# A chunked delta-rule block: chunks of 64 tokens with two sequences in one tile, instead of chunks of 128 tokens

## The chip, the cores and the metric

The kernel runs on one core of a Trainium2 chip. A core has five engines with a queue each: TensorE (PE in the profile; its weight loads are PEld), VectorE (DVE), ScalarE (ACT), GpSimd (POOL) and SyncE (SP), which issues the DMAs here. The metric is the device time of one launch in microseconds, the median of the runs; less is better. All data is float32.

## The reference, cut to what matters

The input x has 8 sequences of 1024 tokens with 128 features. The block is a layernorm, a gated delta-rule attention with 16 heads (keys of 64, values of 128), a layernorm and a residual, and then a small feed-forward part with a token shift. The attention is a recurrence over the tokens, one state S of 64 x 128 per sequence and head:

```python
q = causal_conv_silu(x @ Wq.T, conv_q)      # 4 taps, then l2_norm; k likewise
v = causal_conv_silu(x @ Wv.T, conv_v)
alpha = exp(-exp(A_log) * softplus(x @ Wa.T + dt_bias)); beta = 2 * sigmoid(x @ Wb.T)
def step(S, q_t, k_t, v_t, a_t, b_t):
    kS = einsum('bhd,bhdv->bhv', k_t, S)
    S = a_t * (S - b_t * einsum('bhd,bhv->bhdv', k_t, kS)) + einsum('bhd,bhv->bhdv', k_t, v_t)
    return S, einsum('bhdv,bhd->bhv', S, q_t)
o = rms_norm(o) @ Wo.T
x = x + layernorm(o); x = x + layernorm(ffn(layernorm(x)))
```

## The kernel before, in words

The recurrence is done in chunks of 128 tokens. Inside a chunk the effect of the tokens on each other is a triangular matrix of 128 x 128 per head, whose inverse (`tt`) is formed; between chunks only S is carried. A *unit* is one sequence, half of its tokens (four chunks, 512 tokens) and a group of four heads; there are 8 x 2 x 4 = 64 units, and a tile is one chunk of a unit (256 tiles).

The work is written as generators, one for each stage, that yield before each small part:

- `begins` loads x, normalises and transposes it (`xnT`), and computes the decays (`eg`, `ed`, `ee`, `al`); `keys` and `values` compute seven projections of 512 tokens a unit and convolve them (`conv`: ScalarE copies the product to `pb` and scales it into `acc`, GpSimd keeps the three edge tokens, VectorE adds three taps); `directs` computes the fourth value head by four shifted products that accumulate.
- `lengths` computes norms; `products` loads the decay rows broadcast over the partitions (`at`, `egb`), makes the decay matrix by a scan on VectorE, multiplies keys by keys and queries, and forms `mt` and `at`; `decays` scales the queries on GpSimd.
- `gathers`, `blocks`, `scatters` and `levels` invert the triangular matrix: 16 x 16 blocks on GpSimd (by way of DMAs through DRAM), then on TensorE from 16 to 32, from 32 to 64, and from 64 to 128 (three bursts over `tn`, `mt`, `x64`, `tt`).
- `prepares` transposes the keys, scales them into `kc` and `kd`, and forms `pT` from `kc` and `tt`. `steps` runs the recurrence: `tt` by values into PSUM, plus `pT` by S; ScalarE copies that to `w`; `kd` by `w` updates S on VectorE; queries by S plus `at` by `w` is the output. `norms` copies and scales the output; `projects` multiplies by Wo and ends with the feed-forward part (`ending`).

`Flow.run` (line 177) orders the parts at build time: among the parts whose inputs and buffers are there it takes the one that could start soonest by a small cost table (`Engine.cost`, line 245), and breaks ties by a position that each stage is given (the list at the end: stage, parts per unit, offset). The engines then run the emitted order, each its own queue in sequence; a wait at the head of a queue holds all behind it. All emitted instructions have line 234 in the profile, so groups are told apart by tile names. PSUM is two tiles of two banks (`pair`) and four of one (`bank`); a request for a bank may be given half of a pair, which then is not free for anything else.

Of the kernel before, what the change touches and what calls it, by code (L numbers as in the profile page):

```python
# [19 lines left out]
NP = G // 2  # L20
CU = 4
TU = CU * P
NB = CU * G
NVT = 1
NPAIR = 2
# [9 lines left out]
class Flow:  # L35
# [16 lines left out]
    def __init__(self, nc):  # L52
        self.now = dict(PE=0.0, DVE=0.0, ACT=0.0, POOL=0.0, SP=0.0)
        self.free, self.wrote, self.read = {}, {}, {}
        self.kinds, self.work = {}, [0.0, 0.0]
        self.of = {}
        self.speed, self.window, self.used = 1.0, self.WINDOW, [0.0, 0.0]
        self.pe, self.ve = Engine(self, "PE", nc.tensor), Engine(self, "DVE", nc.vector)
        self.ac, self.po = Engine(self, "ACT", nc.scalar), Engine(self, "POOL", nc.gpsimd)
        self.sp = Engine(self, "SP", nc.sync)  # L60

    @staticmethod
    def region(ap):
# [3 lines left out]
        if ap.space == PSUM:  # L67
            return ap.tensor.name, (0, P, ((0, 1),))
        pitch, parts = ap.ap[0][0], ap.ap[0][1]
        starts, n = [ap.offset % pitch if pitch else ap.offset], 1  # L70
        for s, k in sorted(([s, k] for s, k in list(ap.ap)[1:] if s and k > 1), key=lambda x: x[0]):
            if s <= n or len(starts) * k > 32:
                n = s * (k - 1) + n
            else:
                starts = [x + s * i for i in range(k) for x in starts]
        p0 = ap.start_partition()
# [69 lines left out]
    def give(self, kind, tile_):  # L146
        if tile_.space == PSUM:
            kind, tile_ = self.of.pop(tile_.tensor.name, (kind, tile_))
# [5 lines left out]
    def open(self, kind):  # L154

        have = [(kind, t) for t in self.free.get(kind, ())]
        if kind == "bank" and not have:
            have = [("pair", t) for t in self.free.get("pair", ())]
        return have

    def take(self, kind):
        have = sorted(self.open(kind), key=lambda x: self.ends(x[1]))
        of, t = have[0]
        self.free[of] = [x for x in self.free[of] if x.tensor.name != t.tensor.name]
        if t.space == PSUM:
            self.of[t.tensor.name] = of, t
            if of != kind:
                t = t[:, 0:512]
        return t

    def when_free(self, kind, n, eng):
        have = self.open(kind)
        if len(have) < n:
            return None
        return sorted(self.ends(t, eng) for _, t in have)[n - 1]

    def run(self, streams):
# [6 lines left out]
        while waiting:  # L184
            could = []
            for k, (s, (eng, reads, takes, when, spare)) in enumerate(waiting):
                if when is not None and not when():
                    continue
                if spare > len(self.free["bank"]) + len(self.free["pair"]):
# [34 lines left out]
class Engine:  # L224


    def __init__(self, flow, name, eng):
        self.flow, self.name, self.eng = flow, name, eng
# [16 lines left out]
    def cost(self, op, outs, ins, args, kw):  # L245
# [7 lines left out]
        if self.name == "PE":  # L253
# [8 lines left out]
            if k <= 64 and m <= 64:  # L262
                return 0.105, (0.64, 0.04)
# [34 lines left out]
def kernel(  # L298
# [36 lines left out]
    NC = T // P  # L335
    NH = NC // CU

# [6 lines left out]
    psums = []  # L344
    for kind, n, width in (("pair", NPAIR, 1024), ("bank", 8 - 2 * NPAIR, 512)):
        for i in range(n):
            psums.append(ps.tile([P, width], F32, tag=f"{kind}{i}", name=f"{kind}{i}"))
            give(kind, psums[-1])
# [5 lines left out]
    ident = const.tile([P, G, P], F32, tag="ident", name="ident")  # L354
    for i in range(G):
        make_identity(nc, ident[:, i, :])
    ident1 = ident[:, 0, :]
# [5 lines left out]
    )  # L363
    below = const.tile([P, P], F32, tag="below", name="below")
# [5 lines left out]
    ones = const.tile([P, DK], F32, tag="ones", name="ones")  # L370
    nc.gpsimd.memset(ones, 1.0)
    one = ones[:, 0:1]
# [50 lines left out]
    stock("tn", 1, [P, NB, 2 * BL])  # L423
# [8 lines left out]
    Ss = [mem.tile([P, NP, DV], F32, tag=f"S{g}", name=f"S{g}") for g in range(NG)]  # L432
    edge = mem.tile([P, NT - NG * NVT, KW - 1], F32, tag="edge", name="edge")
    x2T = mem.tile([P, 1 + TU], F32, tag="x2T", name="x2T")

    stock("xnT", 2, [P, KW - 1 + T])
    stock("xs", 1, [P, CU, D])
    for kind, n in (("z", 1), ("e", 1), ("la", 1), ("al", 1), ("nbeta", 2), ("eg", 2), ("ed", 2)):
        stock(kind, n, [P, NC, H])
    stock("ee", 2, [P, NC, H // 2])  # L440
    stock("rows", 1, [NC * H, 2, P])
    stock_dram("rowd", 2, [2, NC * H, P])
# [11 lines left out]
    stock("mt", 2, [P, NB, P])  # L454
# [4 lines left out]
    stock("pb", 2, [P, KW - 1 + TU])  # L459
    stock("vT", 1, [P, TU])  # L460
    stock("at", 9, [P, G, P])
    stock("egb", 2, [P, NP, P])
    stock("kd", 2, [P, G, DK])
    stock("kc", 2, [P, G, DK])
    stock("pT", 3, [P, NP, P])
    stock("xc", 1, [P, NB, BL])
    stock("x64", 1, [P, 2 * G, 2 * BL])
# [15 lines left out]
    def weights():  # L483
# [20 lines left out]
        yield part("SP", mt=2)  # L504
        first, second_ = take("mt"), take("mt")
# [20 lines left out]
        give("mt", first)  # L526
# [50 lines left out]
        give("mt", second_)  # L577

    units = [(b, hf, g) for b in range(B) for hf in range(NH) for g in range(NG)]
# [22 lines left out]

    def begins():
        for b in range(B):
            yield part("SP", xnT=1, rowd=1,
                       when=lambda: prog["keys"] >= (b - 1) * NH * NG + 3 or b == 0)
            xnT, rowd = take("xnT"), take("rowd")
            po.memset(xnT[:, : KW - 1], 0.0)
            for c0 in range(0, NC, CU):
# [3 lines left out]
                sy.dma_start(  # L613
                    xs, x[b, c0 * P : (c0 + n) * P].rearrange("(c p) d -> p c d", p=P)
                )
# [13 lines left out]
                ac.copy(xnT[:, KW - 1 + c0 * P : KW - 1 + (c0 + n) * P], pt[:, : n * P])  # L629
                give("bank", pt)  # L630
                give("xs", xs)

# [3 lines left out]
            for c in range(NC):  # L636
                o = KW - 1 + c * P
                pe.matmul(ab[:, c], xnT[:, o : o + P], wabT, start=True, stop=True)
# [7 lines left out]
            ac.activation(nbeta, ab[:, :, 1, :], AF.Tanh, scale=0.5)  # L646
# [18 lines left out]
            for par in range(2):  # L665
                pe.matmul(
                    pg[par * DK : (par + 1) * DK, 2 * n : 2 * n + n // 2].rearrange("p (c r) -> p c r", c=NC),
                    ones, byp[:, :, :, par], start=True, stop=True,
                )
            yield part("ACT", pg)  # L670
            ac.activation(eg.rearrange("p c h -> p (c h)"), pg[:, 0:n], AF.Exp)
            ac.activation(ed.rearrange("p c h -> p (c h)"), pg[:, n : 2 * n], AF.Exp)
            ac.activation(ee.rearrange("p c r -> p (c r)"), pg[:, 2 * n : 2 * n + n // 2], AF.Exp)
            ac.activation(al, la, AF.Exp)
# [3 lines left out]
            po.memset(al[0:1], 0.0)  # L678
            pr = take("bank")
            yield part("PE", al)  # L680
            for i, t in enumerate((al, eg)):
                pe.transpose(
                    pr[:n, i * P : (i + 1) * P], t.rearrange("p c h -> p (c h)"), ident1
                )
# [3 lines left out]
            sy.dma_start(rowd.rearrange("k n t -> n k t"), rows)  # L688
# [3 lines left out]
            gs[b] = dict(xnT=xnT, nbeta=nbeta, eg=eg, ed=ed, ee=ee, rowd=rowd)  # L692

    def heads_of(u, t):

        b, hf, g = u
        return t[:, hf * CU : (hf + 1) * CU, g * G : (g + 1) * G]


    def conv(n, u, done, m=None):  # L700
# [3 lines left out]
        yield part("PE", bank=1, spare=2, when=lambda: len(done) < 2 and m in loaded)  # L704
        pp = take("bank")
        xT = gs[b]["xnT"][:, KW - 1 + hf * TU : KW - 1 + (hf + 1) * TU]
        pe.matmul(pp, wT[:, m, :], xT, start=True, stop=True)
        yield part("ACT", pp, acc=1, pb=1)
        acc, pb = take("acc"), take("pb")
        ac.copy(pb[:, KW - 1 :], pp)  # L710
        ac.activation(acc, pp, AF.Copy, scale=taps[:, n, KW - 1 : KW])
        give("bank", pp)

        yield part("POOL", *([pb] if hf < NH - 1 else []))
        if hf:
            po.tensor_copy(pb[:, : KW - 1], edge[:, m, :])
        else:
            po.memset(pb[:, : KW - 1], 0.0)
        if hf < NH - 1:
            po.tensor_copy(edge[:, m, :], pb[:, TU:])  # L720
        for j in range(KW - 1):
            yield part("DVE", acc, pb)
            ve.scalar_tensor_tensor(
                acc, pb[:, j : j + TU], taps[:, n, j : j + 1], acc, ALU.mult, ALU.add
# [15 lines left out]
    def lengths():  # L740
        for n, u in enumerate(units):
# [6 lines left out]
            for pr in range(NP):  # L748
                for i in range(2):
# [3 lines left out]
                    ac.activation(qk[:, pr, i], acc, AF.Silu)  # L753
# [50 lines left out]
    def rows():  # L804
        for n, u in enumerate(units):
# [9 lines left out]
            for h in range(G - NVT):  # L815
# [3 lines left out]
                ac.activation(vT, acc, AF.Silu)  # L819
# [16 lines left out]
    def directs():  # L836
        for n, u in enumerate(units):
            b, hf, g = u
            a = st[n]
            for c in range(CU if NVT else 0):  # L840
                t0 = hf * TU + c * P
# [3 lines left out]
                for j in range(KW):  # L845
                    pe.matmul(
                        pv[:, : NVT * DV], xnT[:, t0 + j : t0 + j + P],
                        wv[:, g, j].rearrange("p h v -> p (h v)"), start=j == 0, stop=j == KW - 1,
                    )
# [13 lines left out]
    def decays():  # L863
        for _ in range(len(units) * CU):
# [5 lines left out]
            st[n]["decayed"] = st[n].get("decayed", 0) + 1  # L870
# [5 lines left out]
    def products():  # L876
        def fetch(n, c):
            b, hf, g = units[n]
            yield part("SP", at=1, egb=1, when=lambda: b in gs)
            n0 = (hf * CU + c) * H + g * G  # L880
            at, egb, rowd = take("at"), take("egb"), gs[b]["rowd"]
            sy.dma_start(
                at.rearrange("p h t -> p (h t)"),
                rowd.rearrange("k n t -> k (n t)")[0:1, n0 * P : (n0 + G) * P]
                .broadcast_to([P, G * P]),
            )
            for par in range(2):
                src = rowd[1:2, n0 + par : n0 + G : 2, :]
                sy.dma_start(egb[par * DK : (par + 1) * DK], src.broadcast_to([DK, NP, P]))
# [3 lines left out]
        for n, u in enumerate(units):  # L893
            a = st[n]
            for c in range(CU):
                if ahead is None:
# [4 lines left out]
                atf = at.rearrange("p h t -> p (h t)")  # L901
                ve.tensor_tensor_scan(
                    atf, atf, ident.rearrange("p h t -> p (h t)"), 0.0, ALU.mult, ALU.add
                )
                ahead = None
                k = n * CU + c + 1
# [3 lines left out]
                yield part("PE", pair=1, spare=2, when=lambda: prog["keys"] > n, **takes)  # L910
# [3 lines left out]
                tok = slice(c * P, (c + 1) * P)  # L914
                mt = a["mt"][:, c * G : (c + 1) * G]
# [510 lines left out]
```

## Time and profile before

| | |
|---|---|
| median of 3 runs | 3778.35 us (3777.87 to 3783.65) |
| profiled execution, span | 3779.1 us |
| TensorE busy | 3435.4 us (91%), mean granted clock 0.949 |
| VectorE busy | 2688.5 us (71%) |
| GpSimd busy | 2404.3 us (64%) |
| ScalarE busy | 2311.7 us (61%) |
| DMA | 186.28 MB, mean 49 GB/s |

The page has no other time for the profiled execution than its span. Busy time is the union of an engine's instructions; it says how full an engine is, not that it waits for nothing. "out<-in" names the tile written and those read; for TensorE the numbers before the shape are the rows and columns of the array that the instruction uses (64*128: half of the rows). The mean of one instruction includes its way through the array, so it overlaps with its neighbours; busy time over count, or the step between starts, is what it takes.

### The profile page before, as it was taken

Reading aid. Unit: us, or ns where it says so; the run is one execution under the profiler, and the core shown is the slowest. Engines: PE = TensorE matmul, PEld = TensorE weight load, DVE = VectorE, ACT = ScalarE, POOL = GpSimd, SP = SyncE. Lnnn points to the kernel's source line nnn. Section 1 sums busy time; section 2 is a strip of 40 time slices with the busy share of each in tenths; the row PEclk is TensorE's granted clock in tenths of the full one; section 3 lists DMA queues with packets and bytes.
Section 4 is the critical chain, followed back from the end, with each engine's and each line's share of the span. In section 5 each row is a group of like instructions: output and inputs, shape, how many; then the busy total and the mean of one; then the engine's idle time right before and its main releaser. Section 6 shows DMA issues by size and latency. Waiting matters only on the chain.

```text
span 3779.1 us, 126912 instructions
## 1 busy us (share of the span) xinstructions
PE 3435.4 (91%) x52848; PEld 2646.7 (70%) x52848; DVE 2688.5 (71%) x5021; ACT 2311.7 (61%) x5779; POOL 2404.3 (64%) x4369
## 2 busy tenths in 40 slices
PE   6899998999999999998998989999998989989996
PEld 3677776777777776776766767767776767667775
DVE  5776767677777777866777677777767777777752
ACT  4566656666657666666656656566565666566652
POOL 4666667567666666666566566666666656576662
PEclk8899999999999999999999999999999989999997
DMA  3221222222222222221222222222222222222210
GB/s 80 56 53 39 54 45 49 54 45 55 49 55 46 57 50 43 56 53 40 54 44 53 52 42 53 47 54 51 51 45 55 49 41 60 44 48 53 49 39 11
DMA packets 713151, 186.28 MB, mean 49 GB/s; under 512 B 573152, under 2 KB 679040, under 8 KB 712576
## 3 DMA queue, kind: packets, MB, share of 16 engines
q1 hardware_dynamic: 712576, 178.17, 22.9%
q8 instruction: 415, 6.80, 0.8%
q14 instruction: 160, 1.31, 0.1%
HBM read 138.18 MB, written 23.07 MB: 43 GB/s over the span
## 4 chain that ended last, share of the span: by engine, by line
PE 63%; DVE 10%; POOL 7%; ACT 7%; SPq 6%; issue 5%; DMA 3%; POOLq 0%; DVEq 0%; ACTq 0%
PE bank L234 38%; PE pair L234 25%; SPq L234 6%; DVE acc L234 5%; POOL nb L234 3%; POOL tmp L234 2%; DMA nb<-md 2%; ACT acc L234 1%; DVE x L234 1%; ACT tt L234 1%; DVE at L234 1%; ACT L234 1%; ACT pb L234 1%; POOL vr L234 1%; ACT junk L234 1%
## 5 line engine op out<-in xcount | busy, mean ns | idle before, releaser
L234 DVE SCALAR_TENSOR_TENSOR acc<-pb,taps,acc 128x512 f32<-128x512 f32 x1344 | 1076.1, 806 | 158.2 <-POOL pb L234 64.9
L234 POOL TENSOR_TENSOR vr<-vr,r 128x128 f32<-128x128 f32 (+1 forms) x448 | 353.9, 791 | 252.5 <-ACT vr L234 247.0
L234 PE MATMUL bank<-xnT,wT 128*128 128x512 f32 x892 | 492.4, 641 | 14.8 <-ACT tt L234 8.7
L234 POOL TENSOR_TENSOR nb<-nb,tmp 128x14 f32<-128x14 f32 (+6 forms) x896 | 337.8, 377 | 70.2
L234 ACT COPY pb<-bank 128x512 f32<-128x512 f32 x446 | 259.6, 582 | 161.0 <-PE bank L234 122.1
L234 POOL TENSOR_TENSOR qk<-qk,egb 128x256 f32<-128x256 f32 x256 | 228.4, 892 | 202.5 <-PE pair L234 201.4
L234 ACT COPY o<-pair 128x512 f32<-128x512 f32 x256 | 150.4, 588 | 328.3 <-PE pair L234 286.2
L234 POOL TENSOR_TENSOR tmp<-nb 128x14 f32<-128x14 f32 (+6 forms) x896 | 319.4, 356 | 48.4
L234 DVE TENSOR_TENSOR_SCAN at<-at,ident 128x512 f32<-128x512 f32 x256 | 336.5, 1314 | 12.0 <-DMA at<-rowd 11.7
L234 PEld LDWEIGHTS bank<-tn,mt 32*32 32x32 f32 (+1 forms) x14240 | 276.4, 110 | 97.1 <-issue 22.3
L234 ACT ACTIVATE junk<-o 128x128 f32<-128x128 f32 x1024 | 317.5, 310 | 26.4
L234 PE MATMUL bank<-tn,mt 32*32 32x16 f32 (+1 forms) x14240 | 310.0, 190 | 17.8 <-DVE tn L234 7.6
L234 PE MATMUL pair<-vr,tt 128*128 128x128 f32 x2048 | 292.9, 289 | 26.7 <-ACT tt L234 19.5
L234 ACT ACTIVATE acc<-bank,taps 128x512 f32<-128x512 f32 x446 | 309.7, 694 | 0.3
L234 POOL TENSOR_TENSOR so<-so,es 128x4 f32<-128x4 f32 x256 | 64.2, 251 | 377.7 <-ACT junk L234 377.4
L234 PE MATMUL bank<-woT,oT 128*128 128x128 f32 x2048 | 290.1, 285 | 10.5 <-ACT oT L234 7.2
L234 PEld LDWEIGHTS bank<-wv,xnT 128*128 128x128 f32 x2016 | 257.9, 197 | 57.8 <-issue 36.1
L234 POOL TENSOR_TENSOR o<-o,so 128x512 f32<-128x512 f32 x256 | 284.8, 1112 | 18.0
L234 PEld LDWEIGHTS pair<-vr,tt 128*128 128x128 f32 x2048 | 265.9, 203 | 42.6 <-ACT tt L234 22.1
L234 PE MATMUL pair<-w,at 128*128 128x128 f32 x2048 | 291.8, 287 | 0.2 <-issue 0.2
L234 PE MATMUL bank<-wv,xnT 128*128 128x128 f32 x2016 | 284.7, 286 | 7.4 <-issue 3.5
L234 PEld LDWEIGHTS bank<-woT,oT 128*128 128x128 f32 x2048 | 255.2, 194 | 46.0 <-issue 15.9
(202 smaller groups left out, 7739.1 us busy)
## 6 DMA issues: line engine op xcount, KB each, us to landing
at<-rowd SPq DMA_DIRECT2D x256, 256.0 KB, 3.3
egb<-rowd SPq DMA_DIRECT2D x512, 64.0 KB, 3.2
tq<-td SPq DMA_DIRECT2D x256, 64.0 KB, 2.2
tt<-tq SPq DMA_DIRECT2D x256, 64.0 KB, 2.6
md<-mt SPq DMA_DIRECT2D x512, 16.0 KB, 1.8
nb<-md SPq DMA_DIRECT2D x64, 128.0 KB, 2.8
td<-nb SPq DMA_DIRECT2D x128, 64.0 KB, 3.1
xs<-in_L_attn_x_dram SPq DMA_DIRECT2D x16, 256.0 KB, 3.4
```

What stands on the lines that cost most here:

```text
L234: res = call(*args, **kw)
```

## The change

The chunk is 64 tokens. A tile of 128 partitions holds the same chunk of two sequences side by side: partitions 0 to 63 are one sequence, 64 to 127 the other. A unit is now two sequences, 256 tokens of each, and four heads, so there are 64 units and 256 tiles as before. Sequences go in pairs, each pair in two stretches ("eras") of 512 tokens, with S, the edges of the convolution (`edge`) and the last tokens (`tail`) carried over.

- The inverse needs only 64 x 64 per head and sequence: the three bursts of `levels` from 64 to 128 go, and one of three products at the level before. `tt` stays 128 x 128 with two diagonal blocks, and `tt` by values is unchanged.
- Products that belong to one sequence are 64x64 blocks of TensorE: keys by keys and queries, `kc` by `tt`, queries by S, `pT` by S, `kd` by `w` and `at` by `w`. Shifted products in `directs` and the last two products of the feed-forward part are split by sequence.
- `products`, `decays` and `prepares` handle two tiles at a time. S has one state per sequence, so its update is four operations a tile instead of two, and queries by S moves ahead of the copy to `w`; both outputs of a tile share one PSUM pair, which is held until `norms` has copied the output.
- PSUM is four pairs, each of which can be split into two banks that are given and returned singly; `Flow` books PSUM by bank. Cost table and positions are changed to go with it.

```diff
+X = 2
+C = P // X
 CU = 4
-TU = CU * P
+TS = CU * C
+TU = X * TS
...
-                if spare > len(self.free["bank"]) + len(self.free["pair"]):
+                if spare > len(self.free["bank"]) + 2 * len(self.free["pair"]):
...
             if k <= 64 and m <= 64:
-                return 0.105, (0.64, 0.04)
+                t = n * 0.00168 / self.side * 1.12
+                return t, (1.0, 0.7)
...
-    for kind, n, width in (("pair", NPAIR, 1024), ("bank", 8 - 2 * NPAIR, 512)):
+    for i in range(4):
+        t = ps.tile([P, 1024], F32, tag=f"ps{i}", name=f"ps{i}")
...
-    Ss = [mem.tile([P, NP, DV], F32, tag=f"S{g}", name=f"S{g}") for g in range(NG)]
+    Ss = [mem.tile([P, X, NP, DV], F32, tag=f"S{g}", name=f"S{g}") for g in range(NG)]
...
-        yield part("SP", mt=2)
-        first, second_ = take("mt"), take("mt")
+        yield part("SP", qk=2)
...
+        last = seg == NE * NH - 1
+        yield part("POOL", *([] if last else [pb]))
+        if seg:
+            po.tensor_copy(pb[:, :, : KW - 1], edge[:, m])
...
                 for j in range(KW):
-                    pe.matmul(
-                        pv[:, : NVT * DV], xnT[:, t0 + j : t0 + j + P],
+                    for i in range(X):
+                        pe.matmul(
+                            pv[i * C : (i + 1) * C, : NVT * DV], xnT[:, i, t0 + j : t0 + j + C],
...
+            for i in range(X):
+                sy.dma_start(
+                    at[i * C : (i + 1) * C].rearrange("p h t -> p (h t)"),
...
-            for c in range(CU):
+            for c in range(0, CU, 2):
...
+                for i in range(2):
+                    for pr in range(NP):
+                        for par in range(2):
+                            rows = slice(par * DK, (par + 1) * DK)
+                            for j in range(X):
+                                tok = slice((c + i) * P + j * C, (c + i) * P + (j + 1) * C)
+                                pe.matmul(
+                                    by[j * C : (j + 1) * C, par, i * NP + pr],
+                                    qk[rows, pr, 0, tok], qk[rows, pr, :, tok], start=True, stop=True,
+                                )
...
-            ac.copy(tn[b1, :, BL : 2 * BL], tn[b1, :, 0:BL])
...
-                pe.matmul(p2[b1, col], tq[b1, h], xc[b1, h, :], start=True, stop=True)
...
-            for k in range(3):
-                if k < 2:
-                    yield part("PE", tn[lo], bank=1)
...
-                        pe.matmul(p34[hi, i, :], mt[lo, h, hi], tn[lo, h, :], start=True, stop=True)
...
+                yield part("PE", kc, pair=1, pT=1)
+                pp, pT = take("pair"), take("pT")
+                pps = pp.rearrange("p (x n t) -> p x n t", x=X, t=C)[:, :, : 2 * NP]
+                for h in range(2 * G):
+                    for i, s in enumerate(sides):
                         pe.matmul(
+                            pps[rows_of(h), i, h // 2], kc[s, h, :], tt[s, c * G + h, s],
...
+                    for pt, q, o in ((pss, a["qk"][:, :, 1], toks), (pus, pT[:, i * NP : (i + 1) * NP], sides)):
+                        for h in range(G):
+                            for j, s in enumerate(sides):
+                                pe.matmul(
+                                    pt[s, h % 2, h // 2], q[rows_of(h), h // 2, o[j]],
+                                    S[rows_of(h), j, h // 2, :], start=False, stop=pt is pus,
...
+                    yield part("PE", w, bank=2)
+                    pst = [take("bank") for _ in range(X)]
                     for h in range(G):
+                        for j, s in enumerate(sides):
+                            pe.matmul(
+                                quads(pst[j])[rows_of(h), h // 2, :], kd[s, i * G + h, :], w[s, h, :],
...
+                    for j in range(X):
...
+                            for pr in range(NP):
+                                ve.scalar_tensor_tensor(
+                                    S[:, j, pr, :], S[:, j, pr, :], gs[b]["ee"][:, j, ca, k : k + 1],
...
+                yield part("PE", w)
+                pe.side = 2
+                for h in (0, 2, 1, 3):
+                    for s in sides:
                         pe.matmul(
+                            pss[s, h % 2, h // 2], at[s, c % 2 * G + h, :], w[s, h, :],
+                            start=False, stop=True, skip_group_check=True,
...
-            (weights(), 1000, 0.0), (begins(), 4.75, 1.60), (keys(), 25, 1.30), (lengths(), 16, 1.37), (products(), 16, 2.13),
-            (rows(), 16, 3.17), (directs(), 12, 2.83), (values(), 19, 3.16), (blocks(), 17, 3.23),
-            (decays(), 8, 2.76), (gathers(), 3, 2.60), (scatters(), 3, 2.70), (levels(), 18, 3.74),
-            (prepares(), 16, 3.41), (steps(), 26.5, 3.58), (norms(), 32, 4.34), (projects(), 28.75, 4.29),
+            (weights(), 1000, 0.0), (begins(), 4.81, 1.60), (keys(), 25, 1.30), (lengths(), 16, 1.37), (products(), 8, 2.13),
+            (rows(), 16, 3.17), (directs(), 12, 2.83), (values(), 19, 3.16), (blocks(), 17, 2.7),
+            (decays(), 4, 2.6), (gathers(), 3, 2.60), (scatters(), 3, 2.75), (levels(), 11, 3.0),
+            (prepares(), 8, 3.3), (steps(), 23.25, 3.58), (norms(), 32, 4.34), (projects(), 28.75, 4.29),
```

## The prediction

> **What bounds the kernel now.** I read the page first (busy shares, granted clock, chain), then TensorE's waits, then TensorE's instructions in order of time, then the groups with shapes kept apart. The page:
>
> ```profile
> PE 3435.4 (91%) x52848; PEld 2646.7 (70%) x52848; DVE 2688.5 (71%) x5021; ACT 2311.7 (61%) x5779; POOL 2404.3 (64%) x4369
> ...
> PE 63%; DVE 10%; POOL 7%; ACT 7%; SPq 6%; issue 5%; DMA 3%; POOLq 0%; DVEq 0%; ACTq 0%
> ```
>
> TensorE is busy 3435 us of 3779 and carries 63% of the chain that ended last; it is idle 344 us. No other engine is over 71%, so time taken from TensorE's own work should come off the span until another engine or a chain of waits takes over. Its waits:
>
> ```profile
> PE bank L234 <- ACT tt L234: 61.0, 36, 5.2
> PE bank L234 <- DVE x L234: 31.8, 23, 4.1
> ```
>
> The two largest both lie in `levels`: the copies that fill `tt`, and the `x` products of its 64-wide levels, which the change drops. TensorE in order of time (start, length of a burst):
>
> ```profile
> 1800.32 1.16 PE L234 MATMUL pair<-w,at 128*128 128x128 f32 x8
> 1801.31 1.06 PE L234 MATMUL pair<-vr,tt 128*128 128x128 f32 x8
> 1802.30 0.71 PE L234 MATMUL pair<-S,pT 64*128 64x128 f32 x8
> 1802.85 1.03 PE L234 MATMUL pair<-qk 64*128 64x256 f32 x8
> 1803.93 0.66 PE L234 MATMUL bank<-w,kd 128*64 128x128 f32 x8
> 1804.52 0.44 PE L234 MATMUL bank<-ident,qk 128*128 128x128 f32 x2
> ...
> 1810.30 1.26 PE L234 MATMUL bank<-tn,mt 32*32 32x16 f32 x128
> 1811.49 1.16 PE L234 MATMUL bank<-woT,oT 128*128 128x128 f32 x8
> ...
> 1833.57 1.14 PE L234 MATMUL bank<-tn,mt 64*64 64x64 f32 x16
> 1834.64 1.13 PE L234 MATMUL bank<-xnT,wT 128*128 128x512 f32 x2
> 1835.61 1.05 PE L234 MATMUL bank<-woT,oT 128*128 128x128 f32 x8
> 1836.59 0.27 PE L234 MATMUL bank<-tn,mt 64*64 64x64 f32 x1
> 1836.59 0.27 PE L234 MATMUL bank<-tt,x 64*64 64x64 f32 x1
> ```
>
> A product of the program is two instructions here (448 convolution products are 896). What a burst costs is the step from its start to the next start, since bursts overlap at their ends. A whole-array instruction of 128 columns costs 0.99/8 = 0.124 us. With half the rows (S,pT) it is 0.55/8 = 0.069, with half the columns (w,kd) 0.59/8 = 0.074: two halves run side by side, at 1.7 to 1.8 of the ideal 2. The 16 block instructions at 1833.57, all in one 64x64 corner, cost 1.07/16 = 0.067 for 64 columns. From 1836.59 two opposite corners start together. How many blocks run at once decides this change, and one other burst speaks for four:
>
> ```profile
> 1034.00 1.06 PE L234 MATMUL bank<-acc,pair 128*32 128x512 f32 x8
> 1035.00 0.44 PE L234 MATMUL bank<-ident,qk 128*128 128x128 f32 x2
> ```
>
> Eight instructions of 512 columns, on four column strips of 32, take 1.00 us: 0.125 each, where one alone costs 0.97/2 = 0.485 (xnT,wT). That is 3.9 at a time, each reading its own data.
>
> The clock:
>
> ```profile
> 1263.00:1270.00 7.00, 3.53 (x19) 1.60 (x18) 3.94 (x13) 2.50 (x6) 6.45 (x16) 0.96 0.00 0
> 1270.00:1278.00 8.00, 8.00 (x51) 6.21 (x43) 5.46 (x18) 2.99 (x6) 5.73 (x17) 0.57 0.01 2
> ```
>
> Columns: stretch, its length, busy PE, PEld, DVE, ACT, POOL, granted clock, DMA. A half-idle TensorE is followed by 8 us at 0.57. The mean clock is 0.949.
>
> **The change part by part.** Before and after have 64 units of four tiles. First or last tiles of a sequence fall from 32 of 256 to 16, so a step skipped there runs 3.75 times a unit, not 3.5. Per unit, at full clock, in us:
>
> For a 64x64 block of 128 columns with all four corners in turn I take 0.034: a quarter of 0.124 is 0.031, and S,pT loses 11% against its half (0.069 for 0.062). For 64 columns 0.017, a quarter of 0.067. The trace has no such burst, so the ends are 0.031 (four at once, nothing lost) and 0.069 (two at a time, the S,pT row). I stay near the low end because the strips of 32 reached 3.9.
>
> 1. `levels`: the three bursts of 64x64 blocks go, 3 x 1.07 = -3.21. The third product at the 32-wide level goes too, but the burst at 1830.95 ran three blocks side by side to 1832.09, 1.14 for 96 instructions; the 64 that stay should cost 1.13 to 1.30 like the other 32x32 burst of 64. 0.
> 2. `products`: four bursts (0.96 to 1.08, mean 1.02) become 2 x 32 instructions of half the columns: 2.18 against 4.08, -1.90.
> 3. `prepares`, kc by tt: 3.5 x 0.585 becomes 2 x 32 x 0.017 = 1.09, -0.96.
> 4. `steps`: S by qk (0.65 a burst) and S by pT (0.55) become 7.5 x 16 x 0.034 = 4.08 against 4.20, -0.12. w by kd: 3.75 x 16 x 0.034 = 2.04 against 2.07, -0.03. w by `at` keeps only the two diagonal corners, so two at a time: 4 x 16 x 0.067 = 4.29 against 3.96, +0.3.
> 5. `directs`: 32 whole-array instructions become 64 with half the columns, at the w,kd price: 4.72 against 3.96, +0.76. The same in the last feed-forward products is under 0.1.
>
> Sum -5.16 a unit, -330 us in 64; at the mean clock, /0.949, -348. With the low end, and `at` at 0.062, it is -6.3 or -425; with the high end +4.9, or about +328.
>
> One rule speaks against the small blocks. The Trainium skill, "TensorE: Matmul & The Clock Gate", section "Wait — 56ns, not 53.3ns?", says that matmuls never start closer than about 25 ns. The burst at 1810.30 has 128 starts in 1.19 us, 9.3 ns apart, so this trace contradicts it. By the rule, step 3 would be 2 x 32 x 0.025 = 1.6 and the total some 33 us worse. I use the row.
>
> The other engines, by groups of before (count, busy, mean ns):
>
> ```profile
> L234 DVE TENSOR_TENSOR_SCAN at<-at,ident 128x512 f32<-128x512 f32 x256 | 336.5, 1314 | 12.0 <-DMA at<-rowd 11.7
> L234 DVE SCALAR_TENSOR_TENSOR S<-S,ee,bank 128x128 f32<-128x128 f32 x382 | 114.7, 340 | 99.8 <-PE pair L234 89.6 <-ACT oT L234 4.7 <-ACT xnT L234 3.3
> L234 POOL TENSOR_TENSOR qk<-qk,egb 128x256 f32<-128x256 f32 x256 | 228.4, 892 | 202.5 <-PE pair L234 201.4 <-DMA egb<-rowd 0.9
> ```
>
> DVE: the scan runs 128 times, not 256 (-168); `mt` and `at` products halve (177 + 176, so -176); kc and kd become 256 of 512 elements at 0.69 (-23); `x` goes (-89); the updates of S grow from 384 to 896 at 0.300 busy (+154). Sum -302: 2386. ACT: copies of `tn` (-76) and of 64-row `tt` (-74) go, pT is merged (-8): 2154. POOL: 128 qk products of 512 elements at the 1.11 of o<-o,so, 142 for 228 (-86); edge copies rise from 224 to 336 each way (2 x 112 x 0.30, less 112 memsets of 0.10, +56): 2374. I credit none of it: TensorE's 3095 covers all three, and without that cover POOL is the one that hardly shrinks.
>
> Queues: SP's `at`/`egb` loads fall from 768 to 512, two tiles at a time; x and out transfers double from 48 to 96, with half the rows each; 2064 DMAs in all for 2256. `at` needs two landings (3.3 us median), one pair of tiles ahead. Price 0, hidden behind the work of two tiles.
>
> New waits. The S update is four operations, 4 x 0.34 = 1.36 us where it was 0.68, and S by qk of the next tile, with all that TensorE has queued behind it, waits for it. A tile's chain (S products 1.1, w copy 0.58, w by kd 0.55, update 1.36, some hops) is near 4.2 of the 13.4 us a tile would have: 0, and 0.68 x 240 = 163 if the cover is gone. A tile of `steps` now keeps a PSUM pair until `norms` has copied o, and `prepares` needs a pair: 0, up to one o copy a tile, 256 x 0.59 = 151. At the start the weights borrow two of the three `qk`: 0, up to two weight landings (7.1), 14. On the gain side the DVE x and tn waits (31.8 + 4.7) go; the `tt` copies and POOL's block inverse are late next, so I take -10, at best -37.
>
> Sum: 3779.1 - 348 - 10 = 3421, say 3420. The profiled span is 0.75 us above the median of the runs, 3778.35, so no offset is needed; 0.2% is about what a measurement tells from no change.
>
> **The rivals.**
> - *Cover lost*: TensorE does its work faster and then waits. For it: POOL's 2374 would be 69% of 3420 where it was 64% of the span, and 37% of the chain is not TensorE's. Against it: DVE and ACT shrink with TensorE. One of the two waits above, about 155, in full: 3575.
> - *Clock lower*: if small or diagonal blocks keep the clock down and it falls from 0.949 to 0.92, 3087 x 0.949/0.92 adds 97: 3520. Against: stretches full of 32x32 blocks stand at 1.00.
> - *Better*: four at once without loss, levels' waits gone: 3779 - 425 - 37 = 3315.
> - *Blocks two at a time* (the change does not do what it says): S, kd and products at 0.069. 3435 + 328 = 3763 busy, + 344 idle = 4105. For it: two are all that a 64x64 burst shows, and half-array bursts never show more. Against: the four strips of 32. Between -5.16 at 0.034 and +4.9 at 0.069 the sum is zero at 0.052, 2.4 at a time; above that price the kernel is slower.
>
> **How the numbers follow.** As sized, 3420 with its own range 3350 to 3490: 0.50. Better: 0.15. Clock or cover: 0.25, the hundredth of it near no gain being my "same". Two at a time: 0.10. The range leaves out that last one and some of both tails: 3300 to 3600. Faster 0.89, same 0.01, slower 0.10.
>
> **What would show it.** Right: bursts of 16 instructions (S,pT, w,kd) step 0.5 to 0.6 us, the 32 of products 1.0 to 1.2, kc by tt about 0.55; no 64x64 group of tn,mt; TensorE busy near 3090; DVE near 2390, POOL near 2370; clock 0.94 to 0.96. Wrong: bursts of 16 at 1.1 us (two at a time); TensorE near 3090 but idle over 450, with a wait on S, on w or on PSUM copies at the top (cover); a clock of 0.92 or less.

## The result and the profile after

The changed kernel takes 4035.14 us (median of 4 runs, 4024.99 to 4047.98) where the kernel before took 3781.0 beside it (3777.87 to 3784.84): 1.067 times as long, interval 1.0636 to 1.0706. The forecast was 3420, faster.

The page of the changed kernel, its span, busy times and granted clock by slices:

```profile
span 4046.3 us, 143706 instructions
...
PE 3301.4 (82%) x61712; PEld 2442.9 (60%) x61712; DVE 2427.0 (60%) x4797; ACT 2177.0 (54%) x5427; POOL 2341.8 (58%) x4381
...
PEclk7798999989898799889999999998998888898987
```

TensorE lost work, 3435.4 us busy to 3301.4. But it is idle 4046.3 - 3301.4 = 744.9 us where it was idle 343.7: +401 against -134, which is the +267 between the spans. All engines are less full than before, so no engine has become the bound. At full clock TensorE's work fell by 3435.4 x 0.949 - 3301.4 x 0.887 = 332 us; forecast were 330. (The mean granted clock fell from 0.949 to 0.887.) Busy time times clock is a rough measure: for the same bursts it comes to 2908 to 2963 us in the runs below, against 2928 here, so the saving is known to some 30 us and the agreement to 2 us is luck. The saving came about as worked out, and waits took more than all of it.

TensorE's instructions in order of time, changed kernel (start, length of a burst, rows*columns of the array, count):

```profile
1801.69 1.09 PE L251 MATMUL ps<-w,at 64*64 64x128 f32 x16
1802.71 1.16 PE L251 MATMUL ps<-vr,tt 128*128 128x128 f32 x8
1803.80 0.69 PE L251 MATMUL ps<-tt,kc 64*64 64x64 f32 x32
1804.42 0.66 PE L251 MATMUL ps<-ident,acc 128*128 128x128 f32 x4
1805.01 0.67 PE L251 MATMUL ps<-S,qk 64*64 64x128 f32 x16
1805.50 0.62 PE L251 MATMUL ps<-S,pT 64*64 64x128 f32 x16
1806.04 1.09 PE L251 MATMUL ps<-wv,xnT 128*64 128x128 f32 x16
1807.07 1.13 PE L251 MATMUL ps<-xnT,wT 128*128 128x512 f32 x2
1808.12 0.67 PE L251 MATMUL ps<-w,kd 64*64 64x128 f32 x16
1808.72 0.28 PE L251 MATMUL ps<-ident,cn 128*16 128x128 f32 x1
...
1815.56 1.10 PE L251 MATMUL ps<-qk 64*64 64x128 f32 x31 [0.35 <-issue]
1816.59 0.99 PE L251 MATMUL ps<-tq,xs 32*32 32x16 f32 x96
```

Steps from start to start: 16 blocks of 64x64 in 0.49 (S,qk), 0.54 (S,pT), 0.60 (w,kd); 31 blocks of `products` in 1.03; 32 of 64 columns (tt,kc) in 0.62. A whole-array burst of 8 (vr,tt) has 1.09. So four blocks run at a time, at 0.031 to 0.038 us for 128 columns; `w,at`, on the two diagonal corners, has 1.02 for 16, two at a time.

Who waits longest, changed kernel (time in total, times, longest):

```profile
POOL vr L251 <- ACT vr L251: 589.3, 250, 14.9
...
ACT vr L251 <- PE ps L251: 332.4, 227, 8.6
...
ACT pb L251 <- PE ps L251: 295.7, 199, 6.0
DVE y L251 <- PE ps L251: 225.4, 121, 9.9
```

The same groups in the kernel before:

```profile
ACT vr L234 <- PE bank L234: 155.2, 128, 5.5
...
ACT pb L234 <- PE bank L234: 122.1, 154, 3.8
...
DVE y L234 <- PE bank L234: 105.7, 93, 5.5
```

These three, which read PSUM, now wait two to two and a half times as long for TensorE, though TensorE has less to do. And TensorE's own waits, which were led by `levels` before, are now led by ScalarE's reads of PSUM:

```profile
PE ps L251 <- ACT acc L251: 147.1, 128, 5.4
PE ps L251 <- ACT oT L251: 89.2, 103, 2.8
PE ps L251 <- ACT vr L251: 58.1, 86, 5.2
```

One stretch shows what they wait for. All engines, changed kernel (the bracket is the idle time before an instruction):

```profile
1797.40 1.74 PE L251 MATMUL ps<-xnT,wT 128*128 128x512 f32 x2
...
1807.07 1.13 PE L251 MATMUL ps<-xnT,wT 128*128 128x512 f32 x2
...
1808.12 0.67 PE L251 MATMUL ps<-w,kd 64*64 64x128 f32 x16
1808.23 0.28 ACT L251 ACTIVATE vr<-ps 128x128 f32<-128x128 f32 x1 [1.16 <-PE ps L251]
...
1808.84 0.59 ACT L251 COPY pb<-ps 128x512 f32<-128x512 f32 x1 [0.33 <-PE ps L251]
...
1809.32 0.69 ACT L251 ACTIVATE acc<-ps,taps 128x512 f32<-128x512 f32 x1
...
1810.05 1.13 DVE L251 SCALAR_TENSOR_TENSOR S<-S,ee,ps 128x128 f32<-128x128 f32 x4 [2.69 <-PE ps L251]
```

I set these against the built program, which has the bank that each instruction touches and the semaphore value that it waits for.

- `vr` (1808.23) reads the first half of tile `ps2`. The burst that wrote it (wv,xnT) ended at 1807.13. It starts 0.03 us after the end (1808.20) of xnT,wT, which wrote the *second* half: the value that it waits for is reached only by that second burst.
- `pb` (1808.84) reads the second half of `ps3`, whose data a burst at 1797.40 had written. Its wait is for the w,kd burst, which wrote the *first* half and ended at 1808.79.
- The update of S (1810.05) reads what w,kd had finished at 1808.79 in the first half of `ps3`. It also waits for ScalarE's `acc`, which *reads* the second half until 1810.01. (The profile names TensorE there; the wait that came last is on ScalarE.)

So the waits that are put in when the program is built follow a PSUM tile as a whole, writes and reads alike. The change made all PSUM of two-bank tiles and hands their halves to unrelated work, while `Flow` books each half as free by itself. I counted, in each built program, the waits among TensorE, VectorE and ScalarE in which everything that the awaited step did to a shared tile lies in its other half. It is a lower count: a wait like that of `vr` above, whose awaited step covers both halves, isn't in it.

| kernel | half-only waits, of all | median us |
|---|---|---|
| before | 0 of 8699 | 3781.0 |
| changed | 1715 of 6855 | 4035.1 |

### The profile page after: what moved, and what is told of

Its sections match the earlier page's. It is cut to its first block, busy times and chain, and to the rows that moved or that the text cites. A ratio compares the mean times of both kernels' runs of the same rounds, so it can differ in the third digit from the quotient of the medians.

```text
span 4046.3 us, 143706 instructions
## 1 busy us (share of the span) xinstructions
PE 3301.4 (82%) x61712; PEld 2442.9 (60%) x61712; DVE 2427.0 (60%) x4797; ACT 2177.0 (54%) x5427; POOL 2341.8 (58%) x4381
## 3 DMA queue, kind: packets, MB, share of 16 engines
q14 instruction: 154, 1.26, 0.1%
## 5 line engine op out<-in xcount | busy, mean ns | idle before, releaser
L251 PE MATMUL ps<-xnT,wT 128*128 128x512 f32 x896 | 564.2, 721 | 90.8 <-ACT acc L251 19.7
L251 ACT COPY pb<-ps 128x512 f32<-128x512 f32 x448 | 262.1, 585 | 435.6 <-PE ps L251 295.7
L251 PE MATMUL ps<-woT,oT 128*128 128x128 f32 x2048 | 342.5, 318 | 84.5 <-ACT oT L251 49.0
L251 PEld LDWEIGHTS ps<-woT,oT 128*128 128x128 f32 x2048 | 296.0, 221 | 151.6 <-ACT oT L251 75.8
L251 PE MATMUL ps<-wv,xnT 128*64 128x128 f32 x4096 | 308.8, 298 | 40.6 <-ACT acc L251 18.0
L251 PE MATMUL ps<-vr,tt 128*128 128x128 f32 x2048 | 307.0, 294 | 26.5 <-POOL vr L251 12.1
L251 ACT ACTIVATE acc<-ps,taps 128x512 f32<-128x512 f32 x448 | 311.1, 695 | 0.0
L251 PEld LDWEIGHTS ps<-vr,tt 128*128 128x128 f32 x2048 | 263.0, 200 | 73.4 <-issue 28.2
L251 POOL TENSOR_TENSOR so<-so,mhalf 128x4 f32<-128x4 f32 x256 | 282.5, 1104 | 20.0
L251 PE MATMUL ps<-w,at 64*64 64x128 f32 x4096 | 288.4, 280 | 5.3 <-issue 3.4
```

The source lines that it names most:

```text
L251: res = call(*args, **kw)
```

## The experiments

Theory A: the waits across halves are the cause, and the rest of the change gives what was forecast. Rival B: PSUM is scarcer than before, since a tile of `steps` holds a pair longer. Rival C: the small blocks keep the clock down.

### The changed kernel on the PSUM tiles of before

```diff
-    for i in range(4):
-        t = ps.tile([P, 1024], F32, tag=f"ps{i}", name=f"ps{i}")
+    for kind, n, width in (("pair", 2, 1024), ("bank", 8 - 2 * 2, 512)):
+        for i in range(n):
+            psums.append(ps.tile([P, width], F32, tag=f"{kind}{i}", name=f"{kind}{i}"))
...
-            return ap.tensor.name, (0, P, tuple((x // 512, (x + n + 511) // 512) for x in starts))
+            return ap.tensor.name, (0, P, ((0, 1),))
...
-                if spare > len(self.free["bank"]) + 2 * len(self.free["pair"]):
+                if spare > len(self.free["bank"]) + len(self.free["pair"]):
```

Giving and taking of PSUM are those of the kernel before too, and `spare` (how much PSUM must be free before a new product may start) is 2 for 3.

> The changed kernel with the PSUM of before: two pairs and four single banks, each a tile of its own, and a pair's second half never given to another user. Everything else of the change stays. Theory A (halves of one pair are waited for together, so that a reader of one half waits for TensorE's later burst into the other): the waits go, TensorE idles 350 to 450 us instead of 745, the clock is back at 0.93 to 0.95, and the time is 3400 to 3600. Theory B (PSUM is too scarce, because a step now holds its pair until the output is copied): fewer ways to hand out a bank make it worse, 4050 or more. Theory C (small blocks let the clock fall, and the idle follows from that): the clock stays near 0.89 and the time at 3900 or more.

Measured: 3471.97 us, 0.9189 of the kernel before (0.9163 to 0.9215), and no half-only wait in 7754. Its page, with the chain that ended last (that of the changed kernel breaks off after a few per cent and can't be set against it), and its stretch with the same kind of update:

```profile
PE 3080.2 (89%) x61712; PEld 2322.1 (67%) x61712; DVE 2434.7 (70%) x4797; ACT 2177.7 (63%) x5428; POOL 2410.5 (69%) x4381
...
PEclk8899999999999999899999999999998999999997
...
PE 58%; POOL 12%; DVE 9%; ACT 8%; issue 6%; SPq 2%; DMA 2%; POOLq 0%; DVEq 0%; ACTq 0%
```

```profile
1500.97 0.67 PE L236 MATMUL bank<-w,kd 64*64 64x128 f32 x16
...
1501.76 1.12 DVE L236 SCALAR_TENSOR_TENSOR S<-S,ee,bank 128x128 f32<-128x128 f32 x4
```

The update of S starts 0.12 us after its burst ended (1501.64), not 1.26 after. TensorE is idle 389.5 us and its clock is 0.944, with all small blocks in place, so C falls. TensorE's busy time, 3080.2, is what was forecast (3087 to 3095).

### The kernel before with the splitting pairs

```diff
-    for kind, n, width in (("pair", NPAIR, 1024), ("bank", 8 - 2 * NPAIR, 512)):
-        for i in range(n):
-            psums.append(ps.tile([P, width], F32, tag=f"{kind}{i}", name=f"{kind}{i}"))
+    for i in range(4):
+        t = ps.tile([P, 1024], F32, tag=f"ps{i}", name=f"ps{i}")
...
-            return ap.tensor.name, (0, P, ((0, 1),))
+            return ap.tensor.name, (0, P, tuple((x // 512, (x + n + 511) // 512) for x in starts))
```

Giving, taking and `spare` are those of the changed kernel too.

> The kernel before with one part of the change alone: four pairs that split into banks, booked by bank, and nothing of the 64-token chunks. Theory A: the same false waits appear without any 64x64 block; TensorE idles 600 us or more and the time is 4000 to 4200. Theory B: more freedom in PSUM and no longer holding, so the same or faster, 3700 to 3790. Theory C: no 64x64 block added, so the clock stays near 0.95 and the time near 3780.

Measured: 4296.42 us, 1.1372 (1.133 to 1.1414), with 1784 half-only waits in 7749, TensorE idle 663 us and its clock at 0.906.

```profile
PE 3635.0 (85%) x52848; PEld 2740.4 (64%) x52848; DVE 2688.7 (63%) x5021; ACT 2334.7 (54%) x5783; POOL 2364.5 (55%) x4369
```

The part of the change that has nothing to do with chunks costs the kernel before 516 us by itself, more than the 4000 to 4200 that I expected.

### The changed kernel, PSUM booked whole

The four tiles and their splitting stay; only `Flow` is told that a step touches the whole tile, so it plans with the waits that will be there.

```diff
+        if ap.space == PSUM:
+            return ap.tensor.name, (0, P, ((0, 1),))
...
-        if ap.space == PSUM:
-            return ap.tensor.name, (0, P, tuple((x // 512, (x + n + 511) // 512) for x in starts))
```

> The changed kernel with one function undone: the planner books a PSUM pair as a whole, as before, instead of by bank, so it knows of waits across the halves and orders around them; the halves are still given out singly. Theory A: part of the loss comes back, 3800 to 3950, TensorE idle 500 to 650. Theories B and C: as the changed kernel, within 1% of 4035.

Measured: 3673.38 us, 0.9712 (0.9689 to 0.9735), 1082 half-only waits in 7138, TensorE idle 519 us. 362 of the 563 us between the changed kernel and the one on the tiles of before come back from the order alone. A's expectation had too little for that: most of the harm is that the planner orders work against waits that it doesn't know. What TensorE waits for in this kernel:

```profile
PE ps L251 <- ACT acc L251: 69.7, 76, 5.7
```

### Three fixed pairs, and four pairs given whole

Both are the first experiment with another split of the eight banks: three pairs and two banks, and four pairs with no single bank, where a request for a bank takes a pair and leaves half unused.

```diff
-    for kind, n, width in (("pair", 2, 1024), ("bank", 8 - 2 * 2, 512)):
+    for kind, n, width in (("pair", 3, 1024), ("bank", 8 - 2 * 3, 512)):
```

> As the two fixed pairs, but three pairs and two single banks. Theory A: no false waits either, so under 3750, though two single banks make TensorE queue for PSUM more than with four: slower than two pairs by 50 to 250. Theory B: a third pair is what the held pairs lack, so the fastest of these, and the only one well under 4035.

> The changed kernel with its four pairs, but a request for one bank takes a whole pair and leaves the second half empty. No false waits, and half of PSUM goes unused by the single-bank stages. Theory A: faster than the changed kernel's 4035 although PSUM is far scarcer, 3650 to 3950. Theory B: the slowest of all, over 4035.

Measured: 3687.83 us, 0.9748 (0.9721 to 0.9775), with three pairs; 3677.19 us, 0.9695 (0.965 to 0.974), with four. Neither has a half-only wait. TensorE in the second:

```profile
PE 3158.6 (86%) x61712; PEld 2363.5 (64%) x61712; DVE 2439.3 (66%) x4797; ACT 2182.2 (59%) x5428; POOL 2374.0 (65%) x4381
```

Two things follow. B is not the cause: if `steps` were short of pairs, three or four of them would beat two, and both are some 200 us slower. And fewer separate tiles go with a longer time even without any wait across halves: 216 us with five tiles for six, 205 with four (191 by the ratios to the kernel before). Whether that is the number of tiles itself, the fewer single banks, or the order that the planner makes of them, these two runs don't tell apart. Four tiles given whole, with half a tile wasted at each request for a bank, are still 358 us faster than the changed kernel, which fills the halves.

### The same order, single banks as halves of two tiles

The cleanest test: the first experiment, with its four single banks made as halves of two two-bank tiles. `Flow` still books each half by itself, so every engine has the same instructions in the same order in the same banks; only which waits are put in differs.

```diff
-            return ap.tensor.name, (0, P, ((0, 1),))
+            half = f".{ap.offset % 1024 // 512}" if ap.tensor.name.startswith("bank") else ""
+            return ap.tensor.name + half, (0, P, ((0, 1),))
...
-    for kind, n, width in (("pair", 2, 1024), ("bank", 8 - 2 * 2, 512)):
-        for i in range(n):
-            psums.append(ps.tile([P, width], F32, tag=f"{kind}{i}", name=f"{kind}{i}"))
-            give(kind, psums[-1])
+    for i in range(2):
+        both_banks = ps.tile([P, 1024], F32, tag=f"bank{i}", name=f"bank{i}")
+        for j in range(2):
+            give("bank", both_banks[:, j * 512 : (j + 1) * 512])
```

> The kernel with two fixed pairs, with one thing changed: its four single banks are the halves of two tiles of two banks, no longer four tiles. Every engine's instructions stand in the same order and use the same number of banks at the same points; only the waits differ. Theory A (waits are kept for the tile, not for the half): 3700 to 4050, TensorE busy work as in e1 but idle over 550 us. Theory B or C (scarcity of PSUM, the order, the clock by the blocks): all three are as in e1, so within 1% of 3472.

Measured: 3899.81 us, 1.0285 (1.0245 to 1.0324), 428 us over the first experiment (by the ratios to the kernel before, 0.11 of it, 414). 2172 of 7258 waits are half-only. Its engines, its waits for PSUM, and below them those of the first experiment:

```profile
PE 3232.6 (83%) x61712; PEld 2395.3 (61%) x61712; DVE 2416.8 (62%) x4797; ACT 2179.4 (56%) x5428; POOL 2352.6 (60%) x4381
```

```profile
ACT vr L237 <- PE bank L237: 313.3, 197, 7.4
ACT pb L237 <- PE bank L237: 290.0, 181, 7.6
...
PE bank L237 <- ACT acc L237: 125.4, 121, 5.4
```

```profile
ACT vr L236 <- PE bank L236: 178.9, 184, 5.2
...
ACT pb L236 <- PE bank L236: 111.1, 125, 5.3
...
PE bank L236 <- ACT acc L236: 35.2, 31, 11.0
```

The same three waits grow here as in the changed kernel, with nothing else changed. TensorE is idle 664 us instead of 390, and its clock falls from 0.944 to 0.916 with the same instructions, so the clock follows the waits.

The Trainium skill, "PSUM — Partial Sum Buffer", section "PSUM bank collisions raise a hardware error", asks for semaphores by bank and 32-partition quadrant, reads against reads included, and calls guarding by bank the simple version. The programs here guard by the two-bank tile, which is wider than that rule needs; the run above prices the difference. No run here leaves a guard out.

### Better positions and better prices

Two versions on the tiles of before, to see what is left in the order: one with positions or rates of six stages moved, one with the cost table corrected to durations of the profile (0.0019 for 0.00168 us a column, the scan 0.00228 for 0.00204) and then positions for it. The second also changes two constants by which the planner chooses among the parts (`YIELD` from 4.11 to 5.138, `NEAR` from 0.35 to 0.21), which its expectation doesn't name.

```diff
-(values(), 19, 3.16) ... (decays(), 4, 2.6), (gathers(), 3, 2.60) ... (levels(), 11, 3.0), (prepares(), 8, 3.3) ... (projects(), 28.75, 4.29)
+(values(), 19, 3.008) ... (decays(), 4, 2.565), (gathers(), 3.24, 2.6) ... (levels(), 11, 3.529), (prepares(), 9.36, 3.3) ... (projects(), 28.75, 4.421)
```

> Two fixed pairs as in e1, with positions of six stages moved (levels 0.5 later, prepares' parts 8 to 9.36, values 0.15 earlier, projects 0.13 later, two by less). A look for a version that beats e1: if e1's rest is idle time set by the order, 3350 to 3470; if it is TensorE's 3080 us of work plus unavoidable hops, within 1% of 3472.

> Two fixed pairs as in e1, with four prices of the planner set to what the profiles show (a matmul of 512 columns 0.97 us instead of 0.86, a block by the same rate, a transpose 0.118, the scan 1.40) and positions chosen with these. If the planner's cheap prices cost order: 3330 to 3450, faster than e7; if not, e7 or slower.

Measured: 3375.59 us, 0.8912 (0.8871 to 0.8953), with moved positions, the best of all; 3414.68 us, 0.90 (0.8964 to 0.9036), with corrected prices. The second lies in the range expected of truer prices but isn't the faster one; as positions and two constants changed with the prices, what the prices alone are worth stays open. The best one's page:

```profile
PE 3063.0 (90%) x61712; PEld 2313.6 (68%) x61712; DVE 2456.5 (72%) x4797; ACT 2176.7 (64%) x5428; POOL 2426.1 (71%) x4381
...
PEclk8899999999999999999999899999999999999997
```

TensorE is idle 330 us, at a clock of 0.954 (in the profiled execution, the slowest of four). That is near the 334 us of idle time that the prediction had counted on, but only after positions were moved.

## Why the prediction was wrong

- *Steps 1 to 5, TensorE's bursts: right.* -332 us at full clock, known to some 30 us, -330 forecast. Products 1.03 (1.09 forecast), S,qk 0.49 and S,pT 0.54 and w,kd 0.60 (0.54 each), kc by tt 0.62 (0.54), w by `at` 1.02 (1.07), wv 1.03 (1.18); the 64x64 bursts of `levels` are gone. The Trainium skill, "TensorEngine Tiling (Array Packing)", sections "Available Configurations" and "Key Properties", has 64x64 as four tiles that execute in parallel; 16 blocks in 0.49 to 0.60 us agree.
- *The other engines: near.* VectorE 2427 (2386 forecast), ScalarE 2177 (2154), GpSimd 2342 (2374). Two prices were low: the `qk` products of 512 elements take 1.404 us, not 1.11, and a scan 1.396, not 1.314.
- *The -10 for idle time: wrong, and the step that failed.* It measured +401. Of the 625 us by which the profiled span exceeds the sum of 3421, 411 are this term; the other 214 are busy time, 3301 for the 3087 forecast, because the sum kept the clock at 0.949. The "New waits" paragraph listed the new holds on PSUM pairs and the longer update of S at 0, and priced their cover at 151 and 163. It gave no line at all to the fourth part of the change, the pairs that split. I had read it as bookkeeping by bank. What it needed was one question: by what unit are waits put in? The change made the planner's unit (a bank) smaller and the waits' unit (a tile) larger, and the kernel before had the two equal. Waits by the two-bank tile cost 428 us at a fixed order; the whole change of PSUM, with its giving and `spare`, costs 516 in the kernel before and 563 in the changed one (4035.14 - 3471.97).
- *Cover lost (3575)*: the kind of loss was right, TensorE with less work and more waiting, with PSUM copies at the top as the prediction's last part said it would show. Its mechanisms were not these, and its size, 155, was under half of the 411 us.
- *Clock lower (3520)*: the clock did fall, to 0.887, but as a consequence. The first experiment's 3080 us of work at 0.944 is 3278 at 0.887, so by this estimate the clock makes some 198 us of busy time out of the waits.
- *Blocks two at a time (4105)*: near the measured time and refuted by the bursts. A total that fits a rival is no evidence for it. (By its own prices, 0.069 in steps 2 to 4, its sum comes to +4.5 to +4.7 rather than +4.9, so to some 4080 to 4095; it changes nothing here.)
- Without the split pairs the kernel takes 3471.97, inside the range of 3300 to 3600 and 52 over the forecast: TensorE as forecast, 55 us more idle than forecast, which moved positions then won back.

What stays open: how the 201 us between booking whole (3673) and the tiles of before (3472) divide between fewer tiles and the waits across halves that remain. The four whole pairs, with no half-only wait, are a similar 205 over the tiles of before, but in another order. A version that waits by bank on the four split tiles was not tried, and neither were `spare` and the giving of halves by themselves; the 428 us at a fixed order owe nothing to either.

## What to carry to other kernels

Where a kernel's own scheduler books a buffer in pieces, look up by what unit the waits are put in; if it is the whole tile, make the pieces tiles of their own, or book the tile whole. A part of a diff that "only" regroups buffers needs its own line in the sum: what each reader will wait for, and what will wait for each reader. The sign is an engine that waits longer for a producer that has less to do; then compare the start of the waiting instruction with the end of the burst that wrote its data and with the end of whatever used the rest of the tile.

## What the runs showed of the hardware

- The clock follows TensorE's idle time over the whole span, nearly: 0.954 at 330 us idle, 0.951 at 342, 0.944 at 390, 0.929 at 503, 0.935 at 516, 0.930 at 519, 0.916 at 664, 0.887 at 745, with the same bursts in all eight. In the changed kernel one stretch shows it (columns as in the prediction: stretch, length, busy PE, PEld, DVE, ACT, POOL, granted clock, DMA):

```profile
1783.00:1790.00 7.00, 0.59 (x6) 0.40 (x4) 3.27 (x5) 6.51 (x10) 0.86 (x1) 0.89 0.00 0
1790.00:1798.00 8.00, 6.49 (x43) 4.16 (x44) 3.42 (x5) 2.22 (x4) 5.84 (x9) 0.50 0.01 2
```

Seven us with almost no work on TensorE are followed by 8 us at half clock, so this wait is paid once when it happens and once more in the bursts after it.

- The price of a 64x64 block went with its columns, and no floor for an instruction showed down to 64 columns: 128 columns take 0.031 to 0.038 us with four corners in turn, 64 columns 0.019 (0.62/32). The block of half the columns costs 0.5 to 0.6 of the whole one.
- A GpSimd product of 128x512 took 1.404 us with `egb` and 1.118 as o<-o,so in the same kernel, so its shape alone doesn't give its time.

```profile
L251 POOL TENSOR_TENSOR o<-o,so 128x512 f32<-128x512 f32 x256 | 286.2, 1118 | 14.9
...
L251 POOL TENSOR_TENSOR qk<-qk,egb 128x512 f32<-128x512 f32 x128 | 179.7, 1404 | 81.5 <-PE ps L251 77.5 <-DMA at<-rowa 3.9
```
